# A graph-network stack in two streams: the second stream held eight row blocks behind the first

## The chip, the cores and the metric

The kernel runs on one core of one Trainium2 chip. The metric is the time of one launch on the device, in microseconds (us). The engines are called PE (TensorE, matrix products), DVE (VectorE), ACT (ScalarE) and SP (SyncE, which here only issues DMAs). Lines such as L1053 are lines of the kernel before.

## The reference

Sixteen graphs of 1024 nodes with 64 features, with a 0/1 adjacency matrix each, go through four layers. Each layer normalises, applies a ReLU and adds its result to `x`.

```python
h = relu(layernorm(x)); x = x + layer0(h, adj, mask)   # thinned neighbours, weighted quantiles, MLP
h = relu(layernorm(x)); x = x + (adj + I) @ h / rowsum(adj + I)
h = relu(layernorm(x)); x = x + attention(h)           # 8 heads, 1024 x 1024 scores plus gamma * adj
h = relu(layernorm(x)); x = x + adj @ (h @ W) + b
```

Layer 0 drops some neighbours of each node (by their rank in the row), takes three weighted quantiles over the remaining neighbours for each feature, and puts the result through two small dense layers. It is by far the longest layer. Layer 2 computes a softmax over 1024 keys for each of 1024 queries and 8 heads. The layers of one graph depend on each other; the graphs do not.

## The kernel before, in words

The program is written as two Python generators that are drained in turn while the program is being built. Nothing of this is decided on the chip.

**The first stream, `picks`,** is layer 0. For each of 16 graphs ("elements") it makes 96 steps (8 feature groups, 2 halves of the columns, 6 quantile places). A step n emits `compare(n)` (L798 to L802 on DVE, L821 on PE), `bits(n-1)` and `value(n-2)`. Along with these it emits parts of the tables of a coming group (`group`), the preparation of the next element (`background`: sorting and thinning; `stages`: neighbour masks and thresholds, mostly in the last twelve steps of an element). After an element's last step, `leave` weighs its last results and applies the two dense layers (L1045, L1049), then adds the sum to `xr` (L1053 to L1055) and puts it into `done`. This is called the hand-over here. It uses both buffers of the PSUM tag `pa`, which `compare` needs as well.

**The second stream, `layers`,** first transposes all adjacency matrices to memory (`turned`), then runs layers 1 to 3 of each element (`rest`), as soon as that element is in `done`. Layer 1 is a normalisation and eight row blocks of products with transposed adjacency rows (`weighted`, L1062 and L1071, each after a 512 KB load). Layer 2 has 4 pairs of heads with 8 row blocks of 128 queries; a row block is scores (L1211), a fused addition and minimum on DVE (L1224), exponentials, 16 transposes (L432), and the product with the values (L1238). Layer 3 is again a normalisation and eight products, then the store of the output.

**How the two are woven.** Each step of `picks` yields a number, .42, which is credit for the second stream. Each part of the second stream yields what it costs. A normalisation and the eight products of layer 1 cost 0.5 and 8 × 0.25, its end 0.2; layer 2's start 0.7, each head pair 0.5 and each row block 0.4 + 0.3 + 0.3; layer 3 is 0.5 and 8 × 0.3. Credit is spent until it is used up; when the second stream must wait for `done` it yields None, and the rest of the credit is lost:

```python
two, due = layers(), 0.0
for r in picks():
    due += r
    while due > 0.0:
        due -= next(two) or due
```

After the last step the list `alone` is filled. From then on several helpers take other buffers: transposed rows from `tb` with six buffers in place of `bt` with two, the scores of the second head from `pc`, most accumulators from `pa` in place of `pb`. What remains of the second stream is then emitted to its end. Tags with a single buffer matter to the change: `po` holds the result `o1` of layer 1 and also `o3` of layer 3; `m1` is a tile of 1024 16-bit values in `positions`.

Of the kernel before, what the change touches and what calls it, by code (L numbers as in the profile page):

```python
# [8 lines left out]
F32 = mybir.dt.float32  # L9
# [12 lines left out]
P = 128  # L22
# [16 lines left out]
def tile_preln_adj_stack(  # L39
# [31 lines left out]
    B, N, D = x.shape  # L71
    C = N // P
# [21 lines left out]
    def b2_(name, shape=(P, 512), dt=F32):  # L94
        return sb.tile(list(shape), dt, tag="b2", bufs=6, name=name)
# [11 lines left out]
    alone = []  # L107
# [9 lines left out]
    def small(name, shape, dt=F32, bufs=3):  # L117
        return sb.tile(list(shape), dt, tag="s_" + name, bufs=bufs, name=name)
# [244 lines left out]
    sb = ctx.enter_context(tc.tile_pool(name="sb", bufs=1))  # L363
# [394 lines left out]
    def picks():  # L758
# [10 lines left out]
        def make(el, g, t):  # L769
            gen = group(el, g, t, weights)  # L770
            tables[el.b, g, t] = next(gen)
            if t == 0 and g < NG - 1:
                todo = [(el, g + 1, 0), (el, g + 1, 1)]
            elif t == 0:
                todo = []
            elif g < NG - 1:
                todo = [(el, g + 1, 2), (el, g + 1, 3)]
            else:
                todo = [(el.b + 1, 0, pp) for pp in range(4)] if el.b + 1 < B else []
            n = 0  # L780
            for _ in gen:
                if n % 2 == 1 and todo:
                    o, g2, pp = todo.pop(0)
                    o = els[o] if isinstance(o, int) else o
                    prepare(o, g2, pp)
                n += 1
                yield None
# [4 lines left out]
        def compare(n):  # L792
            b, g, t, q = steps[n]
            el = els[b]
            hs = slice(t * 512, (t + 1) * 512)
            cum, c1, c0 = tables[b, g, t]
            le = a4("le", (P, 4, 512), HP)
            nc.vector.tensor_tensor(le, cum, bc(el.krow[q][:, None, hs], [P, 4, 512]), OP.is_lt)  # L798
            wa = a4("wa", (P, 4, 512), HP)
            nc.vector.tensor_tensor(wa, le, c0, OP.mult)  # L800
            wb = a4("wb", (P, 4, 512), HP)
            last = nc.vector.tensor_tensor(wb, le, c1, OP.mult)  # L802
            while owing:
                owing.pop()(last)
            prep, val = pa("prep"), pa("val")

            rounds = [
                (prep, [sel_w[:, 1, :]] * 4, [wb[:, pp, :] for pp in range(4)]),
                (prep, [sel_w[:, 0, :]] * 4, [wa[:, pp, :] for pp in range(4)]),
            ] + [  # L810
                (val, [el.tab[:, i, 4 * g + pp, :] for pp in range(4)], [le[:, pp, :] for pp in range(4)])
                for i in range(2)
            ]
            nc.tensor.matmul(
                prep, sel_q[:, q, :], el.kq[:, hs], start=True, stop=False, skip_group_check=True
            )

            def made():
                for i, (dst, w, r) in enumerate(rounds):
                    for pp in range(4):  # L820
                        yield nc.tensor.matmul(  # L821
                            dst[32 * pp : 32 * pp + 32, :], w[pp], r[pp], start=i == 2, stop=i in (1, 3),
                            tile_position=(0, 32 * pp), skip_group_check=True,
                        )

            adjoining(made())
            wi = a2("wi")
            nc.scalar.copy(wi, prep)  # L828
            vs = sb.tile([P, 512], F32, tag="v", bufs=7, name="vs")
            act(vs, val, AF.Copy, scale=1.0 / UP)  # L830
            state[n] = [wi, vs]
# [55 lines left out]
        for n in range(last + 2):  # L887
            b, g, t, q = steps[min(n, last - 1)]
            to_go = per - n % per
            if n < last:  # L890
                if q == 0 and n + NQ < last:
                    coming = make(els[steps[n + NQ][0]], *steps[n + NQ][1:3])
                if to_go == per and b + 1 < B:
                    behind = background(b + 1)
                next(coming, None)
                compare(n)
                if to_go == 2 * NQ and b + 1 < B:


                    for _ in behind:  # L900
                        pass
                    els[b + 1] = arrive(b + 1)
                    stages = els[b + 1].stages
                for _ in range(STEPS.get(to_go, 0)):
                    next(stages, None)
            if 0 <= n - 1 < last:
                bits(n - 1)
            next(coming, None)
            if 0 <= n - 2:
                value(n - 2)  # L910
                if (n - 1) % per == 0:
                    while owing:
                        owing.pop()(None)
                    leave(els.pop(steps[n - 2][0]))
                    for _ in stages:
                        pass
            next(behind, None)
            yield .42


    def ranked(b):
# [29 lines left out]
    def background(b):  # L951

        if b == 0 or b % 2 == 1 and b + 1 < B:
            p = (b + 1) // 2
            pairs[p], rankings[p] = [], ranked(2 * p)

        def half():  # L960
            if b % 2 == 1 and b + 1 == B:
                return
            for r in rankings[(b + 1) // 2]:
                if r is None:
                    yield
                elif b:
                    return

        ranking, thinning, n = half(), dilate(b), 0
        going = [ranking, thinning]  # L970
        while going:
            gen = going[n % 3 // 2] if len(going) == 2 else going[0]
            n += 1
            try:
                r = next(gen)
            except StopIteration:
                going.remove(gen)
                if b == 0 and gen is thinning:
                    going.append(els[0].stages)
                continue  # L980
            if r is None:
                yield
            else:
                thinned[b] = r
# [6 lines left out]
    def arrive(b):  # L991
        el = Element()
        el.b = b
        el.stages = stages(el)
        return el
# [96 lines left out]
    def layer1(b, xr):  # L1092
        h = b2_("h1", (P, C, D))
        norm_relu(xr, h, b2_)
        yield 0.5
        o = sb.tile([P, C, D], F32, tag="po", bufs=1, name="o1")
        for i in range(C):
            nc.scalar.copy(o[:, i, :], weighted(turned_rows(b, i, "aT1"), h))
            yield 0.25
        rc = small("rc1", [P, C], bufs=2)  # L1100
        nc.vector.tensor_scalar(rc, degree[:, b * C : (b + 1) * C], 1.0, None, op0=OP.add)
        nc.vector.reciprocal(rc, rc)
        nc.vector.tensor_tensor(o, o, h, OP.add)
        nc.vector.tensor_tensor(o, o, bc(rc[:, :, None], [P, C, D]), OP.mult)
        bad = b2_("bad", (P, C, D), I32)
        nc.vector.tensor_tensor(bad, o, o, OP.not_equal)
        nc.vector.copy_predicated(o, bad, bc(none[:, :, None], [P, C, D]))
        nc.vector.tensor_tensor(xr, xr, o, OP.add)
        yield 0.2
# [144 lines left out]
    def layer3(b, xr):  # L1254
        h = b2_("h3", (P, C, D))
        norm_relu(xr, h, b2_)
        hT = sb.tile([P, N], F32, tag="hT2", bufs=1, name="h3T")
        to_cols(h, hT, slice(0, D))
        ph = pb("ph3", (P, C, D))
        for j in range(C):  # L1260
            nc.tensor.matmul(ph[:, j, :], hT[:D, j * P : (j + 1) * P], w3, start=True, stop=True)
        hid = b2_("hid3", (P, C, D))
        nc.scalar.copy(hid, ph)
        nc.vector.tensor_tensor(xr, xr, bc(b3r[:, None, :], [P, C, D]), OP.add)
        yield 0.5
        o = sb.tile([P, C, D], F32, tag="po", bufs=1, name="o3")
        for i in range(C):
            nc.scalar.copy(o[:, i, :], weighted(turned_rows(b, i, "aT3"), hid))
            yield 0.3
        nc.vector.tensor_tensor(xr, xr, o, OP.add)  # L1270
        nc.sync.dma_start(out[b].rearrange("(c p) d -> p c d", p=P), xr)


    done = {}
# [9 lines left out]

    def layers():
        yield from turned()
        for b in range(B):
            while b not in done:
                yield None
            yield from rest(b)  # L1290


    two, due = layers(), 0.0
# [2 lines left out]
        while due > 0.0:  # L1296
            due -= next(two) or due
    alone.append(True)
    for _ in two:
        pass  # L1300


# [32 lines left out]
```

## Time and profile before

| | us |
|---|---|
| median of 3 runs (12505.96 to 12527.63) | 12517.13 |
| the profiled execution | 12506.5 |
| its span, first to last instruction | 12504.6 |
| hand-over of element 14 (first product of L1045) | 11422.9 |
| hand-over of element 15 | 12096.7 |
| PE busy | 11332.3 |
| DVE busy | 11411.9 |
| ACT busy | 9572.4 |

Busy time is the union of an engine's instructions. A share over the whole span averages stages with different limits, so the stretches between hand-overs are looked at one by one. An arrow behind a row, as in `<-PE y L1049`, names what ended the idle time of that engine ahead of the instruction. Products on PE are pipelined and their ends are modelled, so a PE row near 100% need not be PE at its peak. The granted clock is the share of PE's full clock that was allowed in a stretch.

### The profile page before, as it was taken

The numbers are of one execution on the slowest core, as the hardware profiler recorded it, in microseconds if no ns is written. First come the engines' busy times: TensorE is split into PE (matmuls) and PEld (weight loads), VectorE is DVE, ScalarE is ACT, GpSimd is POOL, SyncE is SP. The second block draws the span as 40 slices with busy tenths as digits, with TensorE's granted clock in tenths as the row PEclk, the third lists the DMA queues.
The fourth block names the chain that finished last, engine by engine and source line by source line (L and its number), as shares of the span: only waits on it lengthen the run. The fifth ranks groups of instructions, "written<-read, shape, count | busy, mean of one in ns | idle before, by whom it ended". The sixth has DMA issues, their size and how long they took to land. (4 is left out here: it accounts for less than half of the span.)

```text
span 12504.6 us, 216870 instructions
## 1 busy us (share of the span) xinstructions
PE 11332.3 (91%) x85683; PEld 5376.8 (43%) x85697; DVE 11411.9 (91%) x17538; ACT 9572.4 (77%) x17160; POOL 3.2 (0%) x20
## 2 busy tenths in 40 slices
PE   3889999999999998999999999999999999999988
PEld 2334444444444444444444444444444444444445
DVE  8999989899998999989899998999989899988863
ACT  4877877778777887778777787777877778787866
POOL 0000000000000000000000000000000000000000
PEclk6999999999999999999999999999999999999989
DMA  7641121211212121121211212122121211201011
GB/s 237 239 135 54 54 76 57 72 62 59 72 56 77 57 66 64 53 80 57 79 52 60 75 55 75 55 69 66 56 73 54 82 55 59 80 31 56 32 51 59
DMA packets 520558, 908.06 MB, mean 73 GB/s; under 512 B 239728, under 2 KB 274672, under 8 KB 519536
## 3 DMA queue, kind: packets, MB, share of 16 engines
q1 hardware_dynamic: 519536, 894.18, 22.2%
q8 instruction: 672, 11.01, 0.4%
q14 instruction: 350, 2.87, 0.1%
HBM read 683.25 MB, written 206.57 MB: 71 GB/s over the span
## 5 line engine op out<-in xcount | busy, mean ns | idle before, releaser
L800 DVE TENSOR_TENSOR wa<-le,c 128x2048 f16<-128x2048 f16 x1536 | 1873.6, 1220 | 216.6 <-PE prep L821 150.1
L714 PE MATMUL px<-valid,cw 128*128 128x512 fp8e4 x8192 | 1961.8, 381 | 0.0
L802 DVE TENSOR_TENSOR wb<-le,c 128x2048 f16<-128x2048 f16 x1536 | 1872.1, 1219 | 0.0
L798 DVE TENSOR_TENSOR le<-cum,krow 128x2048 f16<-128x2048 int16 x1536 | 1868.8, 1217 | 0.4 <-ACT cum L379 0.4
L379 ACT ACTIVATE c<-px,shifts 128x512 f16<-128x512 f32 x2048 | 1424.9, 698 | 225.8 <-PE px L735 107.1
L1224 DVE CUSTOM_DVE_ANT_0 s<-sp,ad 128x1024 f32<-128x1024 f32 (+1 forms) x1024 | 1231.5, 1203 | 293.8 <-PE sp L1211 289.9
L379 ACT ACTIVATE s<-s,nm 128x1024 f32<-128x1024 f32 x1024 | 1185.4, 1158 | 273.9 <-DVE nm L1224 265.6
L714 PEld LDWEIGHTS <-cw 128*128 128x128 f16 x8192 | 800.4, 98 | 1083.3 <-issue 173.0
L1211 PE MATMUL sp<-kT,qT 64*128 64x512 f32 x4096 | 1230.9, 643 | 38.5 <-DVE nm L1224 35.9
L432 PE MATMUL pcols<-identf,s 128*128 128x128 f32 x8192 | 1160.2, 280 | 102.6 <-ACT s L379 64.1
L828 ACT COPY wi<-prep 128x512 f32<-128x512 f32 x1536 | 912.5, 594 | 413.6 <-PE prep L821 348.5
L435 ACT COPY eT<-pcols 128x512 f32<-128x512 f32 x2048 | 1128.6, 600 | 88.5 <-PE pcols L432 84.6
L432 PEld LDWEIGHTS pcols<-identf,s 128*128 128x128 f32 x8192 | 916.5, 141 | 578.6 <-ACT s L379 201.3
L821 PE MATMUL val<-le,tab 128*32 128x512 f16 x12288 | 1110.1, 389 | 23.8 <-ACT wi L828 13.7
L848 DVE SCALAR_TENSOR_TENSOR vs<-pz,vs 128x512 f32<-128x512 f32 x1536 | 1052.1, 685 | 83.4 <-PE pz L841 78.0
L379 ACT ACTIVATE high<-px,shifts 128x512 f16<-128x512 f32 x1024 | 709.2, 693 | 521.2 <-PE px L714 514.9
L1238 PE MATMUL ao<-eT,v 128*64 128x128 f32 x16384 | 1048.9, 277 | 31.7 <-ACT eT L435 26.3
L379 ACT ACTIVATE vs<-val 128x512 f32<-128x512 f32 x1536 | 939.7, 612 | 110.2 <-PE val L821 72.4
L1238 PEld LDWEIGHTS ao<-eT,v 128*64 128x64 f32 x16384 | 900.6, 137 | 280.9 <-ACT eT L435 149.9
L836 DVE TENSOR_SCALAR bit<-wi,to 128x512 int32<-128x512 int32 x1536 | 832.6, 542 | 4.7 <-ACT cw L379 3.6
L821 PE MATMUL prep<-wb,sel_w 128*32 128x512 f16 x6144 | 656.5, 396 | 189.9 <-DVE wb L802 183.7
L841 PE MATMUL pz<-bit,nth 128*128 128x512 bf16 x1522 | 611.1, 402 | 176.7 <-DVE bit L836 116.4
(262 smaller groups left out, 17794.5 us busy)
## 6 DMA issues: line engine op xcount, KB each, us to landing
ad<-in_adj_dram SPq DMA_DIRECT2D x768, 512.0 KB
aT<-adjT SPq DMA_DIRECT2D x256, 512.0 KB
adjT<-aT SPq DMA_DIRECT2D x128, 512.0 KB
md<-sm SPq DMA_DIRECT2D x216, 256.0 KB
sb<-md SPq DMA_DIRECT2D x216, 256.0 KB
rem_d<-rem SPq DMA_DIRECT2D x128, 256.0 KB
left_d<-nb SPq DMA_DIRECT2D x128, 256.0 KB
lr<-left_d SPq DMA_DIRECT2D x256, 128.0 KB
```

Of the source, the lines that this page charges most:

```text
L379: nc.scalar.activation(out_, in_, func, **kw)
L432: nc.tensor.transpose(pt[:, c, :], ad[:, (4 * s + c) * P : (4 * s + c + 1) * P], identf)
L435: nc.scalar.copy(aT[:, 4 * s : 4 * s + 4, :], pt)
L714: yield nc.tensor.matmul(px[pp], w[:, j, :], valid[:, j, :], start=False, stop=j == C - 1, skip_group_check=True,)
L798: nc.vector.tensor_tensor(le, cum, bc(el.krow[q][:, None, hs], [P, 4, 512]), OP.is_lt)
L800: nc.vector.tensor_tensor(wa, le, c0, OP.mult)
L802: last = nc.vector.tensor_tensor(wb, le, c1, OP.mult)
L821: yield nc.tensor.matmul(dst[32 * pp : 32 * pp + 32, :], w[pp], r[pp], start=i == 2, stop=i in (1, 3), tile_position=(0, 32 * pp), skip_gr ...
L848: nc.vector.scalar_tensor_tensor(vs, pz, 80.0, vs, op0=OP.is_equal, op1=OP.mult)
L1211: nc.tensor.matmul(sps[t], qT[t * D : (t + 1) * D, t ^ e, cols], kT[t * D : (t + 1) * D, e, :], start=True, stop=True,)
L1224: nc.vector.tensor_tensor_reduce(ss[e][:, hs], s, ad[:, hs], -1.0, nms[e] if hs.start else 3.0e38, op0=OP.add, op1=OP.min, accum_out=nm,)
L1238: nc.tensor.matmul(ao[e * D : (e + 1) * D, :], v[:, j, e * D : (e + 1) * D], eTs[e][:, j, :], start=j == 0, stop=j == C - 1, tile_position ...
```

## The change

The credit of a step becomes .414 in place of .42. The generator `layers` ends with element 14; element 15 is taken up after the last step of `picks`. At that point what is left of the second stream is emitted, and after its first part and every third one from there, one part of layer 1 of element 15. Then follow the remaining parts of layer 1, and layers 2 and 3 of element 15. So that layer 1 of element 15 and layer 3 of element 14 can be under way together, `o1` takes the tag `m1` when `alone` is set; both tiles have 2 KB a partition. The arithmetic is the same.

```diff
@@ picks
             next(behind, None)
-            yield .42
+            yield .414
@@ layer1
-        o = sb.tile([P, C, D], F32, tag="po", bufs=1, name="o1")
+        o = sb.tile([P, C, D], F32, tag="m1" if alone else "po", bufs=1, name="o1")
@@ layers
-        for b in range(B):
+        for b in range(B - 1):
             while b not in done:
                 yield None
             yield from rest(b)
@@ the end of the program
     alone.append(True)
-    for _ in two:
-        pass
+    xr = done.pop(B - 1)
+    front = layer1(B - 1, xr)
+    for n, _ in enumerate(two):
+        if n % 3 == 0:
+            next(front, None)
+    for stage in (front, layer2(B - 1, xr), layer3(B - 1, xr)):
+        for _ in stage:
+            pass
```

## The prediction

> **What bounds the kernel now.** I read the page's busy times and 40 slices first, then a table of busy time by stage, then who waits for the first operation of the hand-over `leave` (L1053), then VectorE and TensorE in order of time around hand-overs, the last one above all.
>
> ```profile
> PE 11332.3 (91%) x85683; PEld 5376.8 (43%) x85697; DVE 11411.9 (91%) x17538; ACT 9572.4 (77%) x17160; POOL 3.2 (0%) x20
> PE   3889999999999998999999999999999999999988
> DVE  8999989899998999989899998999989899988863
> ```
>
> Two engines are nearly full together, so the bound has to be found stage by stage. Below, each row is a stretch: length, then busy time of PE, weight loads, DVE, ACT, POOL, then granted TensorE clock, DMA share and GB/s.
>
> ```profile
> 4722.00:4800.00 78.00, 60.27 (x455) 29.48 (x453) 72.61 (x117) 41.98 (x80) 0.00 (x0) 0.87 0.23 74
> 4800.00:5320.00 520.00, 483.18 (x3667) 222.48 (x3666) 517.54 (x757) 413.44 (x727) 0.00 (x0) 1.00 0.16 53
> 5400.00:5471.00 71.00, 67.73 (x545) 32.43 (x538) 57.90 (x86) 53.46 (x103) 0.00 (x0) 1.00 0.38 114
> 11422.90:12096.70 673.80, 635.99 (x4996) 299.23 (x4995) 558.94 (x742) 524.60 (x950) 0.00 (x0) 0.98 0.13 41
> 12096.70:12155.90 59.20, 34.85 (x223) 24.30 (x223) 16.15 (x34) 8.89 (x28) 0.00 (x0) 0.59 0.14 44
> 12155.90:12460.00 304.10, 261.88 (x2023) 166.47 (x2024) 98.51 (x224) 211.76 (x387) 0.00 (x0) 0.97 0.18 58
> ```
>
> An element's window of 731 to 763 us has some 520 us in which VectorE never rests (517.54 of 520), then some 150 us before the hand-over in which TensorE is the limit (67.73 of 71), then a thin stretch after it (4722 to 4800) in which neither is full. The last window, which has no next element to prepare, is TensorE's (636 of 674). After the last hand-over 59 us pass with TensorE 59% busy and its clock at 0.59, before layer 2 of the last element begins.
>
> The hand-over itself has a hole. L1053 reads `y`, the end of a chain from weighing through a DMA and two small products:
>
> ```profile
>   PE y L1049: 115.3, 16
> ```
>
> (idle us and times, all sixteen together), and in order of time:
>
> ```profile
> 4713.35 0.69 DVE L555 TENSOR_TENSOR sv<-sv 128x512 f32<-128x512 f32 x1
> 4722.34 0.69 DVE L1053 TENSOR_TENSOR o<-y,b2r 128x512 f32<-128x512 f32 x1 [8.30 <-PE y L1049]
> 4722.95 0.48 DVE L641 TENSOR_SCALAR nr<-m,r_tau 128x1024 int16<-128x1024 int16 x1
> ```
>
> VectorE waits there once an element, 115.3/16 = 7.2 us each. L641 stands between L1053 and L1054, so the order on an engine is not simply that in which the program gives instructions out. And the TensorE rows of the last hand-over:
>
> ```profile
> 12094.48 1.09 PE L1062 MATMUL two<-aT,hid 128*64 128x128 f32 x16
> 12120.57 1.97 PE L1062 MATMUL two<-aT,h 128*64 128x128 f32 x16 [7.49 <-DVE h L412]
> 12141.61 1.98 PE L1062 MATMUL two<-aT,h 128*64 128x128 f32 x16
> 12154.05 1.89 PE L420 MATMUL pt<-identf,h 128*64 128x128 f32 x8 [9.36 <-DVE h L412]
> ```
>
> Layer 1 of the last element runs alone, each product at 1.98 us where the same one took 1.09 among other work, between two normalisations that leave TensorE idle for 7.5 and 9.4 us.
>
> **What the Trainium skill says.** "Perfetto Trace Analysis", section Optimization Strategy: where the most loaded engine changes over time, interleaving the regimes can help; the stage table shows such regimes, and the change moves work between them, not always the right way. Same page, Identifying Performance Opportunities: a repeated gap can mean too few buffers; here `y` and `ph` hold both `pa` accumulators during the hand-over, and the next `prep` comes only at 4722.38, just when L1053 has read `y`. "PSUM — Partial Sum Buffer", Engine vs sequencer instructions: VectorE's queue is strictly first in, first out; the 8.30 us agree, so only what is queued ahead of L1053 can fill the hole. "TensorE: Matmul & The Clock Gate", What's actually happening: an idle TensorE falls to half clock; 1.98 against 1.09 us agrees.
>
> **The change, part by part.** *Rate .42 to .414.* One element of the second stream is 2.7 (layer 1) + 34.7 (layer 2) + 2.9 (layer 3) = 40.3 units; 96 steps give 40.32 before, 39.74 after. The lag grows by 0.56 a window, over 15 windows to about 8: five row blocks (1 unit each) and layer 3. No instruction is added or removed.
>
> A row block costs VectorE 1231.5/512 = 2.4 us of L1224 and some 0.4 of residual sums (0.20 + 0.68 + 2 × 0.42 = 1.72 us over four blocks), and neighbours overlap by a few hundredths, so 2.75; TensorE 2.40 (L1211) + 2.27 (L432) + 2.05 (L1238) + 0.6 for projections, 7.3. Layer 3 costs TensorE 8 × (1.09 + 0.43) + 2 + 2.5, about 16 us, and VectorE 5; layer 1 some 12 and 7.5.
>
> (a) By the last stretch of the windows 7.9 row blocks fewer have been given out. In VectorE's stretches (about 0.7 of the steps: 67 of 96 L798 lie in 4800 to 5320) each saves 2.75, in TensorE's (0.28) 7.3: 7.9 × (0.7 × 2.75 + 0.3 × 7.3) = 15.2 + 17.3, and 2 more since the last window is all TensorE's: about **-34**. Bounds: -22 (all VectorE) and -58 (all TensorE).
>
> (b) The end, from about 12050, where layer 3 of element 14 begins today, to layer 2 of element 15 at 12156: 106 us. Afterwards there lie 7.9 row blocks (five deferred ones, 2.9 in place of layer 3 in the last seven steps; 58 us of TensorE), the rest of the first stream and its hand-over (27), layer 1 (12) and layer 3 (16). At 92% TensorE use (alone a row block reaches 262/304 = 86%, among other work 94%) the row blocks, the first stream and four layer 1 products (90 us of TensorE) take 90/0.92 = 98; some ten more products of both layers, short of cover, 24 at 2.4 us (1.5 for TensorE, the rest their 512 KB loads); a remainder of the normalisation of layer 3, 3; then the uncovered chain from layer 1's last product to layer 2, 11 (12144.7 to 12156). Together 136: **+30**, bounds 20 and 45. The turn-taking is worth the two idle gaps and the half clock above; in a plain sequence the same work would add 5 × 9.5 + 45 us. The SP queue carries 24 loads here, about 60 us of transfers in 136, so it's not the limit; but the hand-over's `z` transfer can queue behind a row-block load that waits for one of three `adj` buffers.
>
> (c) At 14 hand-overs between. Once the lag passes 2.9 (from the sixth), and in proportion before, row blocks stand where layer 3 stood; that is 11.9 full ones. In the TensorE-bound stretch 2.9 units are 21 us instead of 16; of these 5 to 6 us, the 3.3 us idle in 5400 to 5471 absorb about half: +3 each, **+36**. More VectorE work done there is taken off its own stretch: -1.5 each, **-18**.
>
> (d) The hole at L1053. Today the second stream has nothing to offer there: element b-1 is done and element b not yet there. Afterwards row blocks are at hand; hand-over to `y` lasts 14.4 us (4708 to 4722.4), which is 1.5 row blocks at 9.5 us alone, 1.5 × 2.75 = 4.1 us of VectorE work within a 7.2 us wait. At the 11 later hand-overs: **-45**, if they're queued ahead of L1053. Bounds 0 and 7.2 each, -79.
>
> (e) `o1` in tag `m1`: the same 2 KB a partition, no wait, since `m1` is last used in preparing element 15; without it layer 1 would wait for layer 3's `po`. Nothing. The output DMA of element 14 comes later, hidden behind layer 2 of element 15 (300 us).
>
> Sum: -34 + 30 + 36 - 18 - 45 = **-31 us**. The profiled execution took 12506.5 us (span 12504.6, 1.9 around it), 10.6 below the median of 12517.13; I carry the difference to the median: **12486 us**.
>
> **The rivals.** *R1, slower:* the TensorE-bound stretch decides. Each hand-over then costs the full 6 us (+71), and row-block VectorE work lands behind L1053, of which only one L1224 (1.2 us, -13) fills the hole: -34 + 30 + 71 - 18 - 13 = +36, 12553 us. For it: 95% TensorE use there. It passes the measurable bound once a hand-over costs 4 us more than the hole gives back. *R2, no difference:* the hole is filled half as much (-22) and nothing else moves: -8, 12509 us; the end just takes back what the windows give. *R3, much faster:* the hole closes nearly whole (-75), and a busy TensorE at full clock after hand-overs (0.87 in 4722 to 4800) halves (c)'s 36: -34 + 30 + 18 - 18 - 75 = -79, 12438 us. Against it: 14 us hold hardly two row blocks, and both also want `pb`. That the stated lag doesn't arise I exclude by the arithmetic of units.
>
> **How the numbers follow.** Forecast 0.38, R3 0.10, R2 0.25, R1 0.27. A measurement of this kernel tells some 0.2% (25 us) from no change: faster 0.48, same 0.25, slower 0.27. The forecast's own range is 12455 to 12500; across signs 12425 to 12560, from a little beyond R3 to a little beyond R1, which (a)'s and (b)'s bounds also reach.
>
> **What would show it.** Windows 8 to 14 shorter by a few us each, the early ones by about 2; the wait at L1053 down from 115 us to about 70; TensorE rows of layer 3 after L1053 instead of before; 436 to 440 us from the last hand-over to the end, against 408, with (b) ending in layer 2 of element 15. Wrong would be: the L1053 wait unchanged, longer stretches before hand-overs at 97% TensorE, or more than 450 us at the end.

## The result, and the profile after

The changed kernel takes 12569.83 us in the median (12556.43 to 12576.06), the kernel before 12514.97: a ratio of 1.0042, 95% interval 1.0029 to 1.0054. It is slower by 55 us, where 31 us less was forecast. The profiled execution has a span of 12568.0 us, 63.4 more than before. The page's first parts:

```profile
PE 11371.4 (90%) x85697; PEld 5388.2 (43%) x85697; DVE 11422.9 (91%) x17548; ACT 9590.8 (76%) x17178; POOL 3.2 (0%) x20
...
PE   3888989999899998999989999999989999999988
...
DVE  8999989999898999999999998999999999988852
```

The work is the same. VectorE is busy 11 us longer than before and idle 52 us longer; TensorE is busy 39 us longer with the same products. Two points divide the span: the start of step 1530 of the first stream (the 1531st L798) and the first product for layer 2 of element 15 (L1118).

| us | before | after | difference |
|---|---|---|---|
| start to step 1530 | 12049.3 | 12055.1 | +5.8 |
| step 1530 to layer 2 of element 15 | 106.6 | 159.7 | +53.1 |
| layer 2 of element 15 | 315.8 | 320.2 | +4.4 |
| layer 3 of element 15 from L1261 on | 33.0 | 33.0 | 0 |

The forecast had -61 for the first row and +30 for the second. Both failed, by 67 and 23 us. The first row differs somewhat from run to run: three of the runs below (e1, e5, e6) are the same program up to step 1530 and reach it 7.4 us before to 3.7 us after the kernel before. From the hand-over of element 15 to the end it takes 471.3 us; above 450 was named as a sign of being wrong. Yet the hole at the hand-over did close. This is the wait of L1053 after (idle us and times), against 115.3 in 16 before:

```profile
  PE y L1049: 48.7, 9
```

So (d) came true, and more than made good: 67 us less. Something gave it back. The end, in stretches (the columns are those of the table of stretches before):

```profile
12055.10:12154.30 99.20, 90.81 (x788) 52.77 (x783) 59.36 (x102) 67.56 (x130) 0.00 (x0) 1.00 0.25 83
12154.30:12167.40 13.10, 5.41 (x24) 4.70 (x24) 6.18 (x15) 3.55 (x6) 0.00 (x0) 0.60 0.36 144
12167.40:12203.60 36.20, 31.16 (x217) 24.90 (x216) 0.69 (x1) 6.12 (x24) 0.00 (x0) 0.50 0.32 94
12203.60:12214.80 11.20, 1.83 (x9) 1.24 (x8) 8.19 (x17) 1.63 (x4) 0.00 (x0) 0.50 0.02 3
```

The first row holds the row blocks of element 14, the last of the first stream and four products of layer 1: 99.2 us, forecast 98. The last is the chain to layer 2, 11.2 us, forecast 11. Between them stand the normalisation of layer 3 of element 14 (13.1, forecast 3) and twelve products (36.2, forecast 24). TensorE in order of time shows both:

```profile
12153.81 0.49 PE L1247 MATMUL pp<-wproj,aoT 128*128 128x128 f32 x2 [0.41 <-ACT aoT L1245]
12162.00 1.88 PE L420 MATMUL pt<-identf,h 128*64 128x128 f32 x8 [7.70 <-DVE h L412]
12163.81 3.67 PE L1261 MATMUL ph<-w,h3T 64*128 64x64 f32 x16
12167.41 1.97 PE L1062 MATMUL two<-aT,h 128*64 128x128 f32 x16
12169.81 0.69 PE L1071 MATMUL po<-ident,aoT 128*128 128x64 f32 x2 [0.42 <-ACT aoT L1069]
12170.42 1.98 PE L1062 MATMUL two<-aT,hid 128*64 128x128 f32 x16
12172.82 0.69 PE L1071 MATMUL po<-ident,aoT 128*128 128x64 f32 x2 [0.42 <-ACT aoT L1069]
```

Four products of layer 1 (`two<-aT,h`) were still open when TensorE stood idle for 7.7 us, and none ran in the gap: they had been given out behind the start of layer 3 (L420 and L1261), and the first of them runs right after it. Then layer 3's products (`two<-aT,hid`) and these four run one behind the other, 3.0 us apart, at a granted clock of 0.50.

### The profile page after: what moved, and what is told of

It is laid out like the page before. It is cut to its first block, busy times and chain, and to the rows that moved or that the text cites. A ratio compares the mean times of both kernels' runs of the same rounds, so it can differ in the third digit from the quotient of the medians.

```text
span 12568.0 us, 217008 instructions
## 1 busy us (share of the span) xinstructions
PE 11371.4 (90%) x85697; PEld 5388.2 (43%) x85697; DVE 11422.9 (91%) x17548; ACT 9590.8 (76%) x17178; POOL 3.2 (0%) x20
## 5 line engine op out<-in xcount | busy, mean ns | idle before, releaser
L800 DVE TENSOR_TENSOR wa<-le,c 128x2048 f16<-128x2048 f16 x1536 | 1870.3, 1218 | 225.4 <-PE prep L821 189.1
L798 DVE TENSOR_TENSOR le<-cum,krow 128x2048 f16<-128x2048 int16 x1536 | 1866.9, 1215 | 4.1 <-PE val L821 3.7
L848 DVE SCALAR_TENSOR_TENSOR vs<-pz,vs 128x512 f32<-128x512 f32 x1536 | 1048.7, 683 | 93.1 <-PE pz L841 89.8
L1238 PE MATMUL ao<-eT,v 128*64 128x128 f32 x16384 | 1064.1, 277 | 33.7 <-ACT eT L435 28.6
L1238 PEld LDWEIGHTS ao<-eT,v 128*64 128x64 f32 x16384 | 906.8, 137 | 290.6 <-ACT eT L435 148.6
L379 ACT ACTIVATE low<-px,shifts 128x512 f16<-128x512 f32 x1024 | 714.5, 701 | 33.3 <-PE px L726 31.6
```

The source lines that it names most:

```text
L379: nc.scalar.activation(out_, in_, func, **kw)
L848: nc.vector.scalar_tensor_tensor(vs, pz, 80.0, vs, op0=OP.is_equal, op1=OP.mult)
L1238: nc.tensor.matmul(ao[e * D : (e + 1) * D, :], v[:, j, e * D : (e + 1) * D], eTs[e][:, j, :], start=j == 0, stop=j == C - 1, tile_position ...
```

## The experiments

Three questions were open: whether the turn-taking does anything; where the windows lose what the closed hole and the deferred row blocks gain; and what makes the end long. Times in the profile are compared with the kernel before, steps being counted by the starts of L798. "Windows" are the stretches from step 12 of one element to step 12 of the next, counted from 1 (the last ends at step 1530); elements are counted from 0, so that the "window 1" of some expectations, which is element 1, is the second window here. The lag is the credit, in units, by which the second stream is behind its place in the kernel before; a row block is one unit.

**e1, the rate alone.** The end as before, in sequence:

```diff
-            yield .42
+            yield .414
```

> The rate .414 alone; the end is given out as in the kernel before (rest of element 14, then layers 1, 2 and 3 of element 15 in sequence, o1 in po). Windows up to the last hand-over as in the changed kernel (12096.7 us, within 5). Theory A (taking turns helps, by little): after the hand-over five to six row blocks without layer 1 among them (51 us), layer 3 of element 14 with its chain and eight products at 3.0 us (37), then layer 1 of element 15 with its own chain and eight products at 3.0 (32) and the chain to layer 2 (11): 131 against 118 us, so some 13 to 20 us slower than the changed kernel, 12585 us. Theory B (the turns slow the row blocks as much as they save): within 5 us of the changed kernel, 12570 us. The forecast's own reading was 50 us or more slower.

Ratio 1.0042 (1.0027 to 1.0057), 12565.85 us. From step 1530 to the end it needs 516.4 us, the changed kernel 512.9. Theory B holds: the time can't be told from that of the changed kernel. With turns layer 2 of element 15 begins 8.7 us sooner after step 1530 (159.7 against 168.4 us), but layer 2 itself takes 5.2 us more (320.2 against 315.0), so that 3.5 us are left.

**e2, the lag made late.** .42 at first, .392 in the last windows:

```diff
-            yield .414
+            yield .42 if n <= 12 * per else .392
```

> The changed kernel with .42 in the first twelve windows after the first and .392 in the last three, so that the same eight units of lag arise in windows 13 to 15 only. Theory A (small lags of 1 to 3 units cost about 7 us a hand-over, larger ones little or nothing): windows 1 to 12 as in the kernel before, windows 13 to 15 shorter by 5 + 12 + 19 us, the end longer by 63: about 12545 us, 25 faster than the changed kernel. Theory B (every window loses by the lower rate, whatever the lag is): the deferred work is the same, so the time is that of the changed kernel, 12570 us.

Ratio 1.0000 (0.9992 to 1.0009). The condition begins one window earlier than the expectation says (385 steps × 0.028 = 10.8 units), and ten units were left. Up to step 12 of element 12 the windows are as before, within 3.5 us each; the last four are shorter by 4.4, 22.0, 7.0 and 22.7, in all 56 us or 5.6 a unit. The end is longer by 62.7. So deferring pays in the windows if it's done late, and the end takes it back. Theory A is right that the place of the lag matters: the changed kernel spread eight units over fifteen windows and came out with +9.5 us over its windows (-4.1 to +2.8 in e1, e5 and e6) instead of -56.

**e3, the lag made early.** All of it in the second window, then carried:

```diff
-            yield .414
+            yield .337 if per < n <= 2 * per else .42
```

> The changed kernel with .337 in window 1 alone and .42 after it: the lag of eight units arises at once and stays. Theory A (small lags cost, a full lag gains some 2 us a window): window 1 shorter by 30 to 40, windows 2 to 15 together shorter by 0 to 30, the end longer by 63: 12510 to 12545 us. Theory B (a lag costs in every window, as row blocks stand in the TensorE-bound stretch before the hand-over, about 3 us each): windows 2 to 15 together longer by 40: 12585 us.

Ratio 1.0048 (1.0033 to 1.0063). The window in which the lag arises is 24.6 us shorter, 3.1 us a unit, near the 2.75 of VectorE. The fourteen windows after it lose 44, some 3 each. That is theory B's amount, but not at B's place. The table has means over elements 3 to 13: the difference to the kernel before, and VectorE's idle time before and in e3.

| steps of the window | e3 against before, us | VectorE idle, us |
|---|---|---|
| -3 to 9, hand-over | -8.9 | 17.0 to 6.9 |
| 9 to 18 | +1.6 | 2.6 to 6.5 |
| 18 to 36 | +8.3 | 1.0 to 9.5 |
| 36 to 78 | -0.4 | 1.4 to 2.3 |
| 78 to 93, ahead of the next hand-over | +3.3 | 17.0 to 16.7 |

With eight units of lag, layers 3 and 1 and the start of layer 2 fall into steps 12 to 28. One window shows it best. The kernel before, the hand-over and then steps 18 to 36:

```profile
3925.20:4034.40 109.20, 99.69 (x778) 46.51 (x776) 91.63 (x153) 76.17 (x149) 0.00 (x0) 1.00 0.30 95
4102.40:4234.70 132.30, 124.75 (x949) 58.34 (x948) 131.59 (x213) 107.83 (x191) 0.00 (x0) 0.99 0.17 57
```

The same steps in e3:

```profile
3925.10:4021.90 96.80, 92.20 (x723) 44.00 (x722) 93.58 (x146) 81.66 (x147) 0.00 (x0) 1.00 0.19 64
4091.40:4235.30 143.90, 125.83 (x939) 59.17 (x940) 131.80 (x222) 93.72 (x177) 0.00 (x0) 0.92 0.25 81
```

VectorE's work in steps 18 to 36 is unchanged (131.59 and 131.80), and the stretch is 11.6 us longer: idle time alone. TensorE idles more there too (18.1 us against 7.6), and its granted clock is 0.92 against 0.99; whether its slower products in turn keep VectorE waiting was not tested. What VectorE waits for in that second row of e3 (total us, times, longest):

```profile
DVE ve L400 <- ACT sq L379: 3.6, 2, 2.7
DVE gm L1120 <- PE pg L1118: 2.9, 1, 2.9
DVE wa L800 <- PE prep L821: 2.8, 3, 2.0
DVE xr L1270 <- ACT o L1268: 1.4, 1, 1.4
DVE r L405 <- ACT sd L379: 0.7, 1, 0.7
```

Four of the five are operations of a layer's start or end, each queued on VectorE before its input is there. Over elements 3 to 13 such operations make up 5.6 of the 9.4 us of waiting in these steps; in the rest L800 and L848 of the first stream wait for TensorE. In the kernel before, the change of layers lies in steps -4 to 10. There it causes little waiting of its own (`gm` 2.3 us a window, L1103 0.8), beside that of the hand-over in steps -3 to 9:

```profile
DVE o L1053 <- PE y L1049: 5.7, 1, 5.7
DVE wa L800 <- PE prep L821: 4.9, 3, 3.2
DVE w L865 <- PE agg L854: 3.7, 2, 3.4
```

I read this so: the two streams each have a hole, and without a lag the holes lie on top of each other. A lag takes them apart: the row blocks fill the first (-12.4 us in this window), and the second opens in a stretch that had no idle time (+11.6). The idle times show that the waiting has moved; its cause is tested in e9, and borne out in part.

**e4, a lag of two units.**

```diff
-            yield .414
+            yield .399 if per < n <= 2 * per else .42
```

> The changed kernel with .399 in window 1 alone and .42 after it: a lag of two units, most of layer 3, in all later windows, and two units left at the end. Theory A (with layer 3 behind the hand-over each costs about 7 us): windows 2 to 15 together longer by 70 to 100 us, end longer by 5 to 15: 12590 to 12620 us. Theory B (the loss does not depend on the lag, or comes at the end only): 12515 to 12555 us.

Ratio 1.0046 (1.0029 to 1.0063), 12573.2 us: less than theory A's figure, well over theory B's. Windows 3 to 16 lose 70 us, 5 each, and the end only 8.8. With layer 3 just behind the hand-over the hole is hardly filled (steps -3 to 9: -2.1), steps 9 to 18 lose 5.2 and 36 to 93 another 6.1, while 18 to 36 gain 3.1. So a small lag costs more a window than a large one (5 against 3 us), and the changed kernel passes through it: its windows 2 and 4 are longer by 13.2 and 11.4, those from the seventh to the fourteenth shorter by 0 to 5. e1, e5 and e6 show the same two windows, longer by 10 to 16.

**e5, another accumulator at the end.** The changed kernel, with

```diff
-        po = pb("po", (P, D))
+        po = pc_("po", (P, D)) if alone else pb("po", (P, D))
```

> The changed kernel with the small accumulator po of the products of layers 1 and 3 in PSUM tag pc in place of pa once the first stream is over, so that the next product's two need not wait for po. Theory A (the twelve products after layer 3's normalisation, and the eight of the last layer 3, run 3.0 us apart because two and po take turns in the same two accumulators and the short stop keeps TensorE at half clock): pitch 1.5 to 2.3 us, end shorter by 15 to 25 us, 12550 us. Theory B (the pitch is TensorE's own at half clock, 1.98 + 0.69 us and the copy has nothing to do with it): 2.7 us apart at best, 6 us shorter; or no change, if the order stays two, po, two, po.

Ratio 1.0017 (1.0010 to 1.0023), against 1.0042 of the changed kernel: some 31 us, more than theory A said: 18.0 up to layer 2 of element 15, 11.6 in its layer 3. The same products in e5:

```profile
12154.74 1.92 PE L1062 MATMUL two<-aT,hid 128*64 128x128 f32 x16
12156.59 0.69 PE L1071 MATMUL po<-ident,aoT 128*128 128x64 f32 x2
12157.21 1.37 PE L1062 MATMUL two<-aT,hid 128*64 128x128 f32 x16
12158.50 0.43 PE L1071 MATMUL po<-ident,aoT 128*128 128x64 f32 x2
12158.87 1.09 PE L1062 MATMUL two<-aT,hid 128*64 128x128 f32 x16
12159.89 0.43 PE L1071 MATMUL po<-ident,aoT 128*128 128x64 f32 x2
12160.26 1.09 PE L1062 MATMUL two<-aT,h 128*64 128x128 f32 x16
```

`two` of the next product no longer needs a buffer that `po` of this one is to take. The 0.42 us stop goes, the products are back at 1.09 us by the fourth, and the distance falls from 3.0 to 1.4 us.

**e6, another order at the end.** All of layer 1 among the row blocks, layer 2 of element 15 begun after layer 3's normalisation:

```diff
+    heads = layer2(B - 1, xr)
     for n, _ in enumerate(two):
-        if n % 3 == 0:
+        if n < 12:
             next(front, None)
+        elif n > 14:
+            next(heads)
-    for stage in (front, layer2(B - 1, xr), layer3(B - 1, xr)):
+    for stage in (front, heads, layer3(B - 1, xr)):
```

> The changed kernel with another order at the end: all of layer 1 of element 15 is given out with the five row blocks (a part after each), and layer 2 of element 15 begins right after layer 3's normalisation of element 14, a part after each product. Windows as in the changed kernel. Theory A (the end is long because layer 3 of element 14 and half of layer 1 run alone: 13 us chain, 36 us of products at half clock): the eight products and the chain go under layer 2's row blocks, which pay 2 us each, end shorter by 25 to 40 us: 12530 to 12545 us. Theory B (what lies in the end is TensorE work that only moves): within 10 us of the changed kernel.

Ratio 1.0032 (1.0021 to 1.0044), 12547.58 us. From step 1530 to the end 495.8 us, 17 less than the changed kernel: in between. The order at the end had something to give, but less than the accumulators.

**e7, the accumulator without the lag.** The kernel before with the edit of e5.

> The kernel before with po in tag pc once the first stream is over: no lag, 16 products alone at 3.0 us (eight of layer 1, eight of layer 3 of element 15). Theory A (as for e5_po_bank): 1 us less for each, 16 us in all: 12497 us. Theory B: 0 to 5 us.

Ratio 0.9985 (0.9979 to 0.9992), 12490.58 us; the end is 16.3 us shorter, as theory A says in sum. The two stretches with the 16 products lose 20.8 us, 1.3 each, and layer 2 between them takes 4.5 more (320.3 against 315.8), though there is no lag. The remedy works without the lag as well. With both kernels so mended, the lag costs 12530 against 12491 us.

**e8, e2 with e5 and e6.** Rate as in e2, `po` in `pc`, layer 2 begun after `n > 22` since more row blocks are left.

> Lag made in the last windows alone (.392 as in e2_late_lag, where ten units were left rather than eight: seven row blocks and layer 3), the end order of e6_end_order (layer 2 begins after layer 3's normalisation) and po in tag pc. Theory A for both halves: windows shorter by 54 us as in e2_late_lag, end longer by 62 - 30 - 15: a gain of some 35 us against the kernel before, 12477 us. If the end can't be shortened (theory B of the two runs above): 12510 us, as e2_late_lag.

Ratio 1.0001 (0.9993 to 1.0010). The windows gained 45 us, the end lost 54. The gains of e5 and e6 don't add up when more row blocks are left over; why was not followed further.

**e9, normalisations in parts.** e3, with `norm_relu` as a generator (`norm_parts`) that gives credit back twice on the way, in layers 1 to 3, and one such point ahead of `gm`; the sums are unchanged:

```diff
         act(sq, d, AF.Square)
+        yield 0.2
...
         act(sd, ve, AF.Sqrt)
+        yield 0.2
...
-        norm_relu(xr, h, b2_)
-        yield 0.5
+        yield from norm_parts(xr, h, b2_)
+        yield 0.1
```

> e3_early_lag with the normalisations of layers 1 to 3 given out in parts: 0.2 of the credit each after the squares and after the root, and 0.15 ahead of gm, so that what waits for ScalarE or TensorE is given out half a step to a step later; the sums of credit are unchanged. Theory A (a lag costs because the change of layers, with its waits of VectorE, now falls into the stretch in which VectorE is the limit: steps 18 to 36 of a window take 8.3 us longer than before, 9.5 us of them idle, against 1.0): these steps lose 4 to 8 us less a window, windows 3 to 15 together 45 to 90 us shorter than in e3_early_lag: 12490 to 12530 us. Theory B (the stretch is longer by the work itself, more of it on ScalarE and TensorE, or the order on VectorE is not moved by the order of giving out): within 15 us of e3_early_lag, 12560 to 12590 us.

Ratio 0.9994 (0.9985 to 1.0002), against 1.0048 of e3. Windows 1 to 16 are 64 us shorter than in e3, as theory A says in sum. The place is only half what it says: the gain is in steps 9 to 18 (4.6 us a window; VectorE idle 6.5 to 2.9 us), where layer 3 starts: L865, which waited 3.5 us a window for TensorE there, no longer does. Steps 18 to 36 gain 0.7 (idle 9.5 to 8.1). In these the waits of a layer's own operations fall from 5.6 to 3.9 us a window, and those of the first stream stay. Without a lag the same parts shorten the windows by 20 us (e11 below). So it is shown that the way in which a layer's start is given out makes the lag dearer, by some 44 us; what keeps steps 18 to 36 long is not settled.

**e10, the lag in the last two windows, with e5.**

```diff
-            yield .414
+            yield .42 if n <= 14 * per else .372
```

> The changed kernel with .42 until the last two windows and .372 in them (nine units left, made where TensorE is the limit and no lag is carried through VectorE's stretches), po in tag pc, turns at the end as in the changed kernel. Theory A: windows 15 and 16 shorter by 9 times 6 to 7 us, 55 to 60, the end longer by 62 - 31 = 31: 25 to 30 us faster than the kernel before, 8 to 10 faster than e7_before_po_bank: 12482 us. Theory B (with the serial products mended there is nothing left for a lag to fill): 12490 to 12500 us, as e7_before_po_bank or slower.

Ratio 0.9995 (0.9986 to 1.0003), 12508.06 us: theory B. Windows 15 and 16 are 58 us shorter as forecast, but from step 1530 on it takes 57 us more than before, not 31, though the twelve products do run 1.4 us apart. Its last row blocks stand some 12 us apart (their value products, L1238, start at 12077.4, 12089.3, 12101.2 and 12113.4) where layer 2 alone needs 9.5.

**e11 and e12, both remedies, without and with the lag.** The kernel before and the changed kernel, each with `norm_parts` and `po` in `pc`.

> The kernel before, no lag, with the normalisations in parts as in e9_early_split and po in tag pc. Theory A: at the hand-over the change of layers lies in the hole that the hand-over makes anyway, so the parts save little there, 0 to 3 us a window: 12450 to 12490 us. Theory B (the parts come later and the element's first row blocks with them): 12490 us or more.

> The changed kernel with both remedies, the normalisations in parts and po in tag pc, against e11_before_split_bank, which has the same two without the lag. Theory A (the lag is worth nothing even so: what it takes out of VectorE's stretches is 3 us a row block, and each row block costs 9 at the end): windows 2 to 16 shorter by 30 to 50 us, the end longer by 26 where e11's is shorter by 13: 12490 to 12515 us, 15 to 40 slower than e11_before_split_bank (12477). Theory B (the lag was good and only these two losses hid it): 12440 to 12465 us.

e11: 0.9967 (0.9955 to 0.9980), 12477.05 us. e12: 0.9973 (0.9963 to 0.9983), 12476.47 us. Both are faster than either kernel, and they can't be told apart. In e12 the windows 1 to 16 are 54.6 us shorter than in the kernel before (e11: 19.9) and the end is 25.3 longer (e11: 13.3 shorter). The parts alone shorten the windows of the changed kernel by 50 us (e12 against e5), those of the kernel before by 20. So theory A's direction for the end and for the windows is right, and its 15 to 40 us against the lag are not: with both remedies the lag costs nothing that can be measured and brings nothing.

## Why the prediction was wrong

**(a) What deferred work saves** had about the right size where it can be seen nearly alone: 3.1 us a unit in e3's second window, where the shares used give 0.7 × 2.75 + 0.3 × 7.3 = 4.1, and 5.6 in e2's last four, between the 2.75 and 7.3 used for the two engines.

**(d) The hole at L1053** closed as said: 115 to 49 us, forecast about 70. Over the whole hand-over stretch (steps -3 to 9) elements 3 to 13 gain 6.8 us each. One reading of the trace was off, though no sum rests on it: `prep` did not wait for L1053 to read `y`. Its first product (L814) ran at 4722.07, before L1053 began at 4722.34, so it took the accumulator that `ph` had left.

**(c) is the step that failed.** Its +3 us for row blocks ahead of the hand-over was about right (steps 78 to 93: +2.1 in the changed kernel, +3.3 in e3). But it has no term for what layers 3 and 1 cost once they move into VectorE's stretch, and even booked a gain of 18 us there, which no stretch shows (steps 36 to 78: -0.2). Their cost there is waiting: steps 9 to 36 take 5.6 us more in the changed kernel for each of elements 3 to 13, some 60 us in all, and 9.9 in e3; VectorE's work did not grow where it was compared (131.59 and 131.80 us). e9 removes most of this in steps 9 to 18 and little in 18 to 36, whose cause stays open. I had seen the thin stretch from 4722 to 4800 and taken it for a fault of the hand-over only; the change of layers lay in the same place. The small lags of the first windows, booked "in proportion", cost the most: windows 2 and 4 alone 25 us.

**(b), the end,** was +30 and is +53 to layer 2, +57 with layer 2, whose 4.4 us more are not explained (e7 has 4.5 more without a lag). The list of what stands there was right, two terms were mis-sized: layer 3's chain (3 forecast, 13.1 measured, since the products meant to cover it were given out behind it) and the products (24 forecast; 36.2, twelve instead of ten, 3.0 us apart instead of 2.4). I took their loads for what spaces them; e5 shows it was a shared pair of accumulators, at a granted clock of 0.50. The turn-taking, which I credited with closing two gaps, is worth 3.5 us by the profiles and nothing that the times show (e1).

The rival R1 had the sign and nearly the time (12553 us), for another reason: it blamed the TensorE-bound stretch before the hand-over and an unfilled hole. The hole was filled, and that stretch lengthened by 2 us, not 6; that its time came so near was luck. The forecast's wide range ended at 12560, 10 us short.

## What to carry to other kernels

Before one of two interleaved streams is shifted, list the holes of both and ask which of them lie on top of each other: a shared hole is paid once, and the shift that fills one can open the other where the limiting engine had no idle time. Price moved work by what its operations wait for on an in-order queue, not only by their busy time, and look at the lags that are passed through on the way. Where a chain runs alone at the end, check first whether two results that follow each other share a pair of accumulators; that edit was worth more here than the re-ordering.

## What the runs showed of the hardware

A chain of small products that began at half clock, with a stop of 0.42 us every 3.0 us, stayed at a granted clock of 0.50 for all of 36 us (31.16 us of them busy); without the stop the same products were back from 1.98 to 1.09 us after about 5 us (e5). The kernel before and e7 show the same, each product of the last layer 1 at 1.98 us with the stop and at 1.09 from the fourth on without it. So the stops, with the clock that went with them, cost more than three times their own length: 12 × 0.42 = 5 us of stops, and 12 × (3.0 - 1.4) = 19 us of time.
